# Six VectorE operations of a Mamba token in another order: three separate steps over two halves instead of one chain per half

## The chip, the core and the metric

The kernel runs on one core of a Trainium2 chip. The core has five engines, each with an in-order queue of its own: TensorE (matmuls into PSUM, called PE in the profile), VectorE (DVE), ScalarE (ACT), GpSimd (POOL) and SyncE (SP), which here only issues DMA transfers. Engines wait for each other by semaphores: an instruction at the head of a queue that must wait holds everything behind it on that engine. The time is the device time of one launch in microseconds. Before the change the median of three runs is 7580.34 us (7578.54 to 7589.2).

## The reference, cut to what matters

The input is an image batch of 2 x 128 channels x 128 x 128. Four layers follow each other: a Mamba layer (a 3x3 convolution, then a Mamba scan, group norm, SiLU, residual), a density gate, a second Mamba layer of the same kind, and a residual block of two 3x3 convolutions. The change is in the scan of the two Mamba layers. Each pixel has its 128 channels cut into 8 tokens of 16, and the scan runs over these 8 tokens for 32 inner channels with 16 states each:

```python
dt = jax.nn.softplus(jnp.einsum('nlr,dr->nld', dt, dt_proj_w) + dt_proj_b)
A = -jnp.exp(A_log)
dA = jnp.exp(dt[..., None] * A)
dBx = dt[..., None] * Bm[:, :, None, :] * xc[..., None]
def step(h, inp):
    a, b, c = inp
    h = a * h + b
    return (h, jnp.sum(h * c[:, None, :], axis=-1))
```

## The kernel before

`_program` (L1028) runs `_mamba`, `_gates`, `_mamba` and `_basic_block`. `_mamba` (L289) works through 64 tiles of 512 pixels (four image rows) for each layer, 128 in all. In a tile the 32 x 16 states of a pixel lie on 128 partitions in four blocks (NJ = 4), so a state tensor of one token is 128 x 4 x 512; it is handled in two halves (`jp` = 0 and 1) of 128 x 2 x 512.

For each token t of 1 to 7 four engines work together:

- `load` (L429, SP's queue) brings `ur` and `bcr` of the token from DRAM, replicated over partitions. `ur` has 3 buffers, `bcr` 5.
- `inject` (L442, GpSimd, L445) multiplies them into `h[t]`, what is added to the state. `h` has 4 buffers.
- `decay` (L447) forms the factor a: eight TensorE matmul instructions (L454) write the exponent of the two halves into two PSUM tiles called `set`, four into each, and ScalarE takes the exponential in place (L463), one instruction for each half. The pool `ps_set` (L298) has three such tiles, used in turn.
- `token` (L465, VectorE) does three operations for each half: L472 multiplies a by h[t-1], in place in the `set` tile; L473 multiplies that by the C part of `bcr` into `r`, which has two buffers; L477, left out for the last token, adds it to h[t]. All three read or write the `set` tile, and the last of them lets it go.
- `gather` (L485, TensorE, L492) sums `r` over the states into the PSUM tile `ys`; after four tokens `gate` (L501, VectorE, L505) takes it over, and `out` projects the result (L512). `spread` (L523, VectorE) takes the statistics of a finished tile.

In between run the first steps for tiles further ahead: convolution taps (L323), transposes (L339), projections (L350, L364, L400), the token's own part (L420), and on ScalarE their copies, the SiLU (L357) and the softplus (L368) with table loads.

The order in each queue is written out by hand: every step of tile k gets a position, k * 7 plus a constant of the list at L268 to L286 (one unit is a token), all steps are sorted by it, ties by the order in which they were put, and emitted (`put`, L554, to L597). `decay` of token t stands at t - 1.2, `token` at t - 1 for half 0 and t - 0.5 for half 1, `gather` at t + 0.35; the two gates at 3.79 and 7.39, the statistics at 12.5. Nothing else is changed about who waits for whom: the semaphores follow from which instruction reads and writes which buffer.

Of the kernel before, what the change touches and what calls it, by code (L numbers as in the profile page):

```python
# [27 lines left out]
ALU = mybir.AluOpType  # L28
# [3 lines left out]
P = 128  # L32
NT, FT = 8, 16
# [8 lines left out]
NS = ROWS * P  # L42
# [237 lines left out]
STORE_AT = -4.15  # L280
LOAD_AT, INJECT_AT = -3.7, -1.8
REP_AT = -1.2
SUM_AT = 0.35
D_AT = (1.25, 4.2)
V_AT = (3.79, 7.39)
# [3 lines left out]
def _mamba(tc, src, w, con, dst, scratch, stats, H):  # L289


    nc = tc.nc
# [11 lines left out]
    live = {}  # L304
# [157 lines left out]
        for x in a:  # L462
            nc.scalar.activation(x, x, AF.Exp)  # L463

    def token(k, t, jp):  # L465

        s = live[k]
        if jp == 0:
            s["r", t] = st.tile([P, NJ, NS], F32, tag="r", name="r", bufs=2)
        pt = s["a", t][jp]  # L470
        js = slice(2 * jp, 2 * jp + 2)
        nc.vector.tensor_tensor(pt, pt, s["h", t - 1][:, js, :], ALU.mult)  # L472
        nc.vector.tensor_tensor(  # L473
            s["r", t][:, js, :], pt, s["bc", t - 1][:, 1].unsqueeze(1).to_broadcast([P, 2, NS]), ALU.mult
        )
        if t < NT - 1:
            nc.vector.tensor_tensor(s["h", t][:, js, :], pt, s["h", t][:, js, :], ALU.add)  # L477

    def through(k, g):

# [73 lines left out]
    def put(k, at, f, *args):  # L554
        at = early.get((k, f, *args), k * SPAN + at)
        todo.append((at, len(todo), f, (k, *args)))


    for k in range(len(src) * ntile):
        if k * ROWS % BAND == 0:  # L560
            put(k, BAND_AT, band)
        for tap in range(9):
            put(k, CONV_AT[tap], conv, tap)
        put(k, TURN_AT, turn)
        for n in range(4):
            put(k, IN_AT[n], project, *divmod(n, 2))
        for name in ("xc", "zs"):
            put(k, SILU_AT, silu, name)
        for i in range(2):
            put(k, BC_AT[i], inout, i)  # L570
        for g in range(2):
            put(k, DT_AT[g], step, g)
        put(k, SOFTPLUS_AT, softplus)
        put(k, PROD_AT, product)
        put(k, U_AT, scaled)
        for g in range(2):
            put(k, OWN_AT[g], own, g)
        put(k, OWN_U_AT, own_u)
        put(k, STORE_AT, store)
        for t in range(NT - 1):  # L580
            put(k, LOAD_AT + t, load, t)
            put(k, INJECT_AT + t, inject, t)
        for t in range(1, NT):
            put(k, REP_AT + t, decay, t)
            for jp in range(2):
                put(k, t - 1 + jp / 2, token, t, jp)
            put(k, SUM_AT + t, gather, t)
        for g in range(2):
            put(k, D_AT[g], through, g)
            put(k, V_AT[g], gate, g)  # L590
        put(k, OUT_AT, out)
        put(k, STATS_AT, spread)
        put(k, KEEP_AT, keep)
# [434 lines left out]
def _program(ctx, tc, d, cols, out):  # L1028
# [7 lines left out]
    with tc.tile_pool(name="const", bufs=1) as cp, tc.tile_pool(name="wts", bufs=1) as wp:  # L1036
        cc = cols["const"]
        ct = cp.tile([P, cc["neghalf"][1]], F32, tag="ct", name="ct")
        nc.sync.dma_start(out=ct, in_=d["const"])
        con = {k: ct[:, a:b] for k, (a, b) in cc.items()}  # L1040
        w1 = cp.tile([P, CG], F32, tag="w1", name="w1")
        nc.sync.dma_start(out=w1, in_=d["w1t"])
        w2 = cp.tile([CG, 2 * P + P // 2], F32, tag="w2", name="w2")
        nc.sync.dma_start(out=w2, in_=d["w2b"])
        b1 = cp.tile([CG, 1], F32, tag="b1", name="b1")
        nc.sync.dma_start(out=b1, in_=d["b1"])
        wm = {"w1": w1, "w2": w2[:, :P], "b2": w2[:, P : 2 * P], "one": w2[:, 2 * P :]}

        y = [dram.tile([P, H, P], F32, tag=f"y_{b}", name=f"y_{b}") for b in range(B)]

        def layer(src, n):
            w = _layer_weights(nc, wp, {k: d[f"L{n}_{k}"] for k in ("conv", "fold", "alog", "keep")}, cols[n], con)
            stats = wp.tile([P, B, H // ROWS, 6], F32, tag="stats", name="stats")
            _mamba(tc, src, w, con, y, scratch, stats, H)
            return w, stats

        x = [d["x"][b] for b in range(B)]
        w, stats = layer(x, 0)
        _gates(tc, x, w, con, y, stats, wm, b1, d["up"], x2, H)
        w, stats = layer(x2, 2)  # L1060
        with tc.tile_pool(name="ps_n", bufs=1, space=PSUM) as pp:
            norm = [_norm(nc, npool, pp, w, con, stats, b) for b in range(B)]
# [44 lines left out]
```

## Time and profile before

| | us |
|---|---|
| median of three runs | 7580.34 |
| the profiled execution, its span from first to last instruction | 7571.5 |
| VectorE busy | 7011.8 (93%) |
| TensorE busy (matmuls) | 6319.0 (83%) |
| GpSimd busy | 5499.8 (73%) |
| ScalarE busy | 4282.3 (57%) |
| L472, L473, L477 on VectorE together | 6254.0 |

In the profile a group is one line of the kernel on one engine: output and inputs by tile name, shape, count, then the busy time in us and the mean of one in ns, then the time that the engine was idle just before such an instruction, and what ended most of it. A line of the order of time gives the start in us from the beginning of the span, the duration, engine, line and operation; a bracket behind it is the idle time ahead of it and what ended it. Durations on VectorE overlap a little at their ends, so starts are compared with starts. In a line of stretches each engine has its busy time in the order PE, PEld, VectorE, ScalarE, GpSimd; then come the granted TensorE clock as a share of full speed, the mean busy share of the 16 DMA engines and GB/s.

The first Mamba layer runs up to about 3300 us, the second from about 3600 to 6900 us.

### The profile page before, as it was taken

How to read it: one execution, taken by the hardware profiler on the slowest of the kernel's cores; microseconds unless marked ns; L12 is line 12 of the kernel's file. 1: busy time of each engine (PE TensorE's matmuls, PEld its weight loads, DVE VectorE, ACT ScalarE, POOL GpSimd, SP SyncE). 2: the span in 40 equal slices, each digit the busy share in tenths (PEclk: the TensorE clock that was granted, in tenths of full speed). 3: DMA queues.
4: the chain of work that ended last, by engine and by line, in shares of the span. 5: the costliest groups of instructions: out<-in, count | busy, mean ns of one | idle time of the engine just before them, and what ended most of it. 6: DMA issues, size and time to landing. Idle time of an engine off the chain costs nothing.

```text
span 7571.5 us, 89536 instructions
## 1 busy us (share of the span) xinstructions
PE 6319.0 (83%) x30416; PEld 2335.1 (31%) x30416; DVE 7011.8 (93%) x7114; ACT 4282.3 (57%) x4877; POOL 5499.8 (73%) x1783
## 2 busy tenths in 40 slices
PE   7888888888888888867788888888888888887994
PEld 2222222222222222224222222222222222223873
DVE  5999999999999999978699999999999999999986
ACT  5666666666656656545556666666656655662222
POOL 5878777877787778754578777877787778775541
PEclk8999999999999999978899999999999999997997
DMA  8999999999999999954799999999999999996604
GB/s 204 252 251 252 251 250 246 256 251 253 246 248 254 250 243 249 245 194 173 193 249 247 250 250 249 250 256 246 249 252 252 251 245 253 249 253 199 207 7 172
DMA packets 573738, 1769.80 MB, mean 234 GB/s; under 512 B 85568, under 2 KB 239712, under 8 KB 458208
## 3 DMA queue, kind: packets, MB, share of 16 engines
q1 hardware_dynamic: 568672, 1747.28, 88.1%
q10 hardware_dynamic: 4608, 16.78, 0.6%
q8 instruction: 242, 3.96, 0.2%
q14 instruction: 216, 1.77, 0.1%
HBM read 1552.83 MB, written 210.89 MB: 233 GB/s over the span
## 4 chain that ended last, share of the span: by engine, by line
DVE 41%; DMA 25%; PE 19%; issue 7%; ACT 5%; POOL 2%; SPq 1%; POOLq 0%; DVEq 0%; ACTq 0%
DMA bcr<-sb 19%; DVE set L472 14%; DVE h L477 12%; DVE r L473 12%; PE m L911 6%; DMA ur<-su 3%; PE one L350 2%; PE set L454 2%; ACT set L463 2%; PE ys L492 2%; PE one L400 2%; POOL h L445 2%; DVE v L505 1%; PE ys L483 1%; ACT xc L357 1%
## 5 line engine op out<-in xcount | busy, mean ns | idle before, releaser
L445 POOL TENSOR_TENSOR h<-ur,bcr 128x2048 f32<-128x2048 f32 x896 | 4060.7, 4539 | 1257.0 <-DMA bcr<-sb 1096.1
L472 DVE TENSOR_TENSOR set<-set,h 128x1024 f32<-128x1024 f32 x1792 | 2193.5, 1224 | 267.6 <-ACT set L463 165.4
L473 DVE TENSOR_TENSOR r<-set,bcr 128x1024 f32<-128x1024 f32 x1792 | 2194.5, 1225 | 61.5
L463 ACT ACTIVATE set<-set 128x1024 f32<-128x1024 f32 x1792 | 1745.9, 1006 | 870.0 <-PE set L454 856.6
L477 DVE TENSOR_TENSOR h<-set,h 128x1024 f32<-128x1024 f32 x1536 | 1866.0, 1215 | 28.1 <-POOL h L445 27.8
L454 PE MATMUL set<-dt,rep 32*128 32x512 f32 x7168 | 1402.9, 675 | 104.9 <-DVE h L477 98.1
L492 PE MATMUL ys<-r,ct 128*32 128x512 f32 x7168 | 1172.5, 635 | 36.4 <-DVE r L473 36.1
L323 PE MATMUL one<-band,conv 128*128 128x512 f32 x2304 | 1081.3, 605 | 21.9 <-DMA band<-in_x_dram 12.6
L454 PEld LDWEIGHTS set<-dt,rep 32*128 32x128 f32 x7168 | 405.1, 193 | 1002.3 <-issue 468.1
L400 PE MATMUL one<-xc,keep 128*64 128x512 f32 x1008 | 322.4, 723 | 462.1 <-ACT xc L357 355.5
L323 PEld LDWEIGHTS one<-band,conv 128*128 128x128 f32 x2304 | 406.6, 189 | 668.0 <-issue 596.8
L911 PE MATMUL m<-comb,u 128*128 128x256 f32 x2304 | 507.8, 381 | 46.0 <-DVE comb L904 44.8
L483 PE MATMUL ys<-t,ct 128*128 128x512 f32 x512 | 322.6, 716 | 252.3 <-DVE v L505 250.7
L911 PEld LDWEIGHTS m<-comb,u 128*128 128x128 f32 x2304 | 436.2, 190 | 117.3 <-issue 54.5
L492 PEld LDWEIGHTS ys<-r,ct 128*32 128x32 f32 x7168 | 181.2, 112 | 929.2 <-issue 759.6
L352 ACT ACTIVATE xc<-one,keep 128x512 f32<-128x512 f32 x252 | 173.4, 688 | 509.2 <-PE one L350 504.2
L374 POOL TENSOR_TENSOR u<-dt,xc 128x1024 f32<-128x1024 f32 x128 | 302.8, 2365 | 98.0 <-ACT dt L368 98.0
L420 PE MATMUL one<-prod,ct 128*128 128x512 f32 x504 | 280.8, 640 | 109.1 <-POOL prod L412 78.8
L350 PE MATMUL one<-y,w_in 128*128 128x512 f32 x504 | 341.1, 765 | 1.6 <-ACT xc L352 1.6
L463 ACT ACT_TABLE_LOAD x254 | 325.9, 1283 | 4.5
L427 POOL TENSOR_TENSOR t<-t,xc 128x1024 f32<-128x1024 f32 x128 | 302.4, 2363 | 10.0
L364 PE MATMUL one<-xc,w_dt 128*128 128x512 f32 x504 | 306.4, 692 | 2.7 <-ACT bc L407 2.7
(167 smaller groups left out, 5901.7 us busy)
## 6 DMA issues: line engine op xcount, KB each, us to landing
ur<-su SPq DMA_DIRECT2D x896, 896.0 KB, 11.5
bcr<-sb SPq DMA_DIRECT2D x896, 448.0 KB, 11.7
ur<-su SPq DMA_DIRECT2D x896, 128.0 KB, 11.1
su<-u SPq DMA_DIRECT2D x1024, 64.0 KB, 3.4
sb<-bc SPq DMA_DIRECT2D x256, 224.0 KB, 2.7
bcr<-sb SPq DMA_DIRECT2D x896, 64.0 KB, 11.0
y<-o SPq DMA_DIRECT2D x128, 256.0 KB, 9.3
band<-in_x_dram SPq DMA_DIRECT2D x28, 640.0 KB, 10.9
```

The source lines that it names most:

```text
L323: nc.tensor.matmul(py.rearrange("p (r w) -> p r w", r=ROWS), lhsT=w["conv"][:, tap, :], rhs=xb[:, r + kh : r + kh + ROWS, kw : kw + P], st ...
L350: nc.tensor.matmul(p, lhsT=w[("in", "z")[i]][:, g, :], rhs=s["y"], start=True, stop=True)
L400: nc.tensor.matmul(p[g * NQ * DS : (g + 1) * NQ * DS, :], lhsT=w[("xb", "xcm")[i]], rhs=s["xc"][:, g, :], start=True, stop=True,)
L445: nc.gpsimd.tensor_tensor(b, s["ur", t], s["bc", t][:, 0].unsqueeze(1).to_broadcast([P, NJ, NS]), ALU.mult)
L454: nc.tensor.matmul(a[j // 2][:, j % 2, :], lhsT=w["rep"][r, q, :], rhs=s["dt"][r, g, :], start=True, stop=True, tile_position=(r.start, 0),)
L463: nc.scalar.activation(x, x, AF.Exp)
L472: nc.vector.tensor_tensor(pt, pt, s["h", t - 1][:, js, :], ALU.mult)
L473: nc.vector.tensor_tensor(s["r", t][:, js, :], pt, s["bc", t - 1][:, 1].unsqueeze(1).to_broadcast([P, 2, NS]), ALU.mult)
L477: nc.vector.tensor_tensor(s["h", t][:, js, :], pt, s["h", t][:, js, :], ALU.add)
L483: nc.tensor.matmul(s["ys", g], lhsT=con["ident"], rhs=s["t1"][:, g, :], start=True, stop=False)
L492: nc.tensor.matmul(s["ys", g][a : a + NQ * DJ, :], lhsT=red[:, q, :], rhs=r[:, j, :], start=False, stop=(q == NQ - 1), tile_position=(0, a),)
L911: nc.tensor.matmul(m[:, n // 2, n % 2], lhsT=u[:, i, kw, :], rhs=v[:, i, :, kw : kw + P], start=(kw == 0), stop=(kw == 2),)
```

## The change

`token` is taken apart into three functions, `decayed` (the line of L472), `weighted` (L473) and `update` (L477). Each has its own positions for the two halves, so that the six operations of a token are spread over one token's time, and the `update` of half 1 falls behind the first operation of the next token. The operands, shapes and the number of operations stay. The `r` buffer of a token is now taken in `weighted`.

```diff
+TOKEN_AT = (("decayed", (0.0, 0.5)), ("weighted", (0.34, 0.84)), ("update", (0.67, 1.17)))
...
-    def token(k, t, jp):
+    def decayed(k, t, jp):
+
+        s = live[k]
+        pt = s["a", t][jp]
+        nc.vector.tensor_tensor(pt, pt, s["h", t - 1][:, 2 * jp : 2 * jp + 2, :], ALU.mult)
+
+    def weighted(k, t, jp):
 
         s = live[k]
         if jp == 0:
             s["r", t] = st.tile([P, NJ, NS], F32, tag="r", name="r", bufs=2)
-        pt = s["a", t][jp]
-        js = slice(2 * jp, 2 * jp + 2)
-        nc.vector.tensor_tensor(pt, pt, s["h", t - 1][:, js, :], ALU.mult)
         nc.vector.tensor_tensor(
-            s["r", t][:, js, :], pt, s["bc", t - 1][:, 1].unsqueeze(1).to_broadcast([P, 2, NS]), ALU.mult
+            s["r", t][:, 2 * jp : 2 * jp + 2, :],
+            s["a", t][jp],
+            s["bc", t - 1][:, 1].unsqueeze(1).to_broadcast([P, 2, NS]),
+            ALU.mult,
         )
-        if t < NT - 1:
-            nc.vector.tensor_tensor(s["h", t][:, js, :], pt, s["h", t][:, js, :], ALU.add)
+
+    def update(k, t, jp):
+
+        s = live[k]
+        h = s["h", t][:, 2 * jp : 2 * jp + 2, :]
+        nc.vector.tensor_tensor(h, s["a", t][jp], h, ALU.add)
...
             put(k, REP_AT + t, decay, t)
-            for jp in range(2):
-                put(k, t - 1 + jp / 2, token, t, jp)
+            for f, at in TOKEN_AT:
+                for jp in range(2):
+                    if f != "update" or t < NT - 1:
+                        put(k, t - 1 + at[jp], {"decayed": decayed, "weighted": weighted, "update": update}[f], t, jp)
             put(k, SUM_AT + t, gather, t)
```

## The prediction

> **What bounds the kernel now.** I read the page's engine rows and costliest groups first, then the waits, then the order of time on single engines in one Mamba tile. I write D, W and U for the three VectorE operations of a token half (L472, L473, L477), with the half (0 or 1) and the token: D0(3).
>
> ```profile
> PE 6319.0 (83%) x30416; PEld 2335.1 (31%) x30416; DVE 7011.8 (93%) x7114; ACT 4282.3 (57%) x4877; POOL 5499.8 (73%) x1783
> ...
> L472 DVE TENSOR_TENSOR set<-set,h 128x1024 f32<-128x1024 f32 x1792 | 2193.5, 1224 | 267.6 <-ACT set L463 165.4
> L473 DVE TENSOR_TENSOR r<-set,bcr 128x1024 f32<-128x1024 f32 x1792 | 2194.5, 1225 | 61.5
> ...
> L477 DVE TENSOR_TENSOR h<-set,h 128x1024 f32<-128x1024 f32 x1536 | 1866.0, 1215 | 28.1 <-POOL h L445 27.8
> ```
>
> VectorE is the busiest engine; 1792 / 14 = 128 tiles carry the three groups. It waits little. In all waits:
>
> ```profile
> PEld set L454 <- DVE h L477: 335.7, 346, 1.4
> ...
> DVE set L472 <- ACT set L463: 165.4, 185, 9.3
> ...
> PE set L454 <- DVE h L477: 98.1, 166, 4.0
> ```
>
> The columns are the total, the times and the longest. Two rows say that TensorE already waits 434 us in front of L454 for a U. Those matmuls write into the `set` ring of three PSUM tiles; U is the last reader of the tile that they want. This is the second loop of the stage: U ends, L454 fills the tile, ScalarE takes the exponential (L463), D reads it.
>
> Five consecutive tiles, by stretches, from D0(1) to D0(1), last 48.95, 51.42, 50.10, 50.89, 48.95; four make the repeating 201.37 us, 50.34 a tile. VectorE rows of the first (start, duration):
>
> ```profile
> 1029.64 1.23 DVE L472 TENSOR_TENSOR set<-set,h 128x1024 f32<-128x1024 f32 x1
> 1030.91 1.22 DVE L473 TENSOR_TENSOR r<-set,bcr 128x1024 f32<-128x1024 f32 x1
> 1032.05 1.21 DVE L477 TENSOR_TENSOR h<-set,h 128x1024 f32<-128x1024 f32 x1
> 1033.18 0.68 DVE L505 TENSOR_TENSOR v<-ys,zs 128x512 f32<-128x512 f32 x1
> ```
>
> W starts 1.26 after the D whose result it reads; the next operation starts 1.14 after W, 1.13 after U, 0.60 after a gate or a statistic. D leads by 0.13 too much. In this tile VectorE never waits: it is the bound. In the others the granted TensorE clock is lower and D0(6), D0(7) wait 0.8 to 1.1 for the exponential:
>
> ```profile
> 1029.64:1078.59 48.95, 42.06 (x181) 13.53 (x182) 48.47 (x45) 31.26 (x36) 39.62 (x11) 1.00 0.98 256
> 1078.59:1130.01 51.42, 45.48 (x183) 13.99 (x186) 48.72 (x44) 30.46 (x36) 40.20 (x13) 0.90 0.97 245
> ```
>
> (the last three columns are clock, DMA share and GB/s).
>
> **What is gained.** By the listed positions the new order on VectorE is D0(t) U1(t-1) W0(t) D1(t) U0(t) W1(t). Two pairs per tile stay dependent: in token 1 there is no U1 of a token before, in token 7 no U0, so W follows its D there. That is 12 shortened D per tile. What an operation behind a D that it doesn't depend on costs, this stage doesn't show. The nearest rows are in the last block, where 256-element operations on PSUM stand 0.33 apart:
>
> ```profile
> 7105.61 0.42 DVE L926 TENSOR_TENSOR sd<-m,c 128x256 f32<-128x256 f32 x1
> 7106.07 0.43 DVE L927 TENSOR_TENSOR sd<-m,c 128x256 f32<-128x256 f32 x1
> 7106.41 0.68 DVE L931 TENSOR_TENSOR Y<-m,sd 128x512 f32<-128x512 f32 x1
> ```
>
> Here L926 and L927 write the PSUM one of the two `sd` tiles. L927, into the same tile, starts 0.46 later; L931, which reads the other `sd` and writes Y, 0.34. So the extra 0.13 belongs to the same tile, not to writing PSUM, and the interleaved neighbour is of another tile: I take 1.13 (bounds 1.13 and 1.26). The Trainium skill speaks against it: VectorE: DVE Perf Modes, "The DRAIN you can't avoid" and "Rules for kernel authors", say that the flush comes after each operation whatever the chaining, so only the number of operations counts. By it the gain is 0; by the rows 12 x 0.13 = 1.56 a tile, 200 us in 128 tiles. The 1.26 against 1.14 in this trace decides for the rows.
>
> **What is lost: the ring.** No engine's operations change in number, no DMA is added. But U moves back. U0 ended 1.26 + 1.14 + 1.22 = 3.62 after its D0 began. Now it is the fifth of six: for tokens 2 to 7 1.13 + 1.13 + 1.14 + 1.13 + 1.22 = 5.75, for token 1 (with the gate between) 1.26 + 1.14 + 0.60 + 1.13 + 1.22 = 5.35. U1 likewise ends two operations later. Tile 2t+1 of the ring takes over tile 2t-2, so the second half of L454 for token t waits for U0(t-1), and everything queued behind it on TensorE waits too: output, convolution taps, projections, the gathers, the next L454.
>
> VectorE alone, token by token with these spacings: 6.40, 6.80, 6.80, 7.40 (gate), 6.80, 7.40 (statistic), 5.80 = 47.40, against 48.95. Now the loop, with TensorE's rows:
>
> ```profile
> 1032.22 2.32 PE L454 MATMUL set<-dt,rep 32*128 32x512 f32 x8
> 1034.47 2.05 PE L512 MATMUL po<-keep,v 128*128 128x128 f32 x16
> ...
> 1040.97 1.14 PE L454 MATMUL set<-dt,rep 32*128 32x512 f32 x8
> ...
> 1064.26 1.12 PE L350 MATMUL one<-y,keep 128*128 128x512 f32 x2
> ```
>
> *Place A, D0(3).* U0(1) ended at 1033.26 and L512 started 1.21 later; from there to the next L454 TensorE had 6.50 of work without a free stretch worth naming (L512, L420, L483, L323, L492). L463 starts 1.17 after L454, D 1.04 after L463: 2.21. From D0(1) the new D0(3) is therefore not before 5.35 + 1.21 + 6.50 + 2.21 = 15.27. VectorE alone would be there at 13.20: a new wait of 2.07. Before, the same chain gave 3.62 + 1.21 + 6.50 + 2.21 = 13.54, under VectorE's 14.73, so it cost nothing.
>
> *D0(4) to D0(6)* are VectorE's: 22.07, 29.47, 36.27. The same sum for them (U0(3) to D0(5): 5.75 + 1.1 + 4.4 + 2.2 = 13.4 against 14.2) leaves under 1 us free.
>
> *Place B, D0(7).* U0(5) ends at 29.47 + 5.75 = 35.22, TensorE goes on at 36.33 (1.11, as behind another blocked L454). Before, it went on at 1064.26; the rows on ScalarE after that:
>
> ```profile
> 1066.18 0.60 ACT L354 COPY zs<-one 128x512 f32<-128x512 f32 x1
> 1066.81 1.28 ACT L357 ACT_TABLE_LOAD   x1
> ...
> 1072.23 1.93 ACT L463 ACTIVATE set<-set 128x1024 f32<-128x1024 f32 x2
> ```
>
> The chain L350, copy, table load, silu, L400, copy, table load, exponential made D0(7) possible at 1072.23 + 1.04, 9.01 after L350. The copy stood behind two exponentials; now the first is long done, and it can start 1.15 after L350 instead of 1.92: 8.24 remain. D0(7) is at 44.57, VectorE alone 43.67: a wait of 0.90. Then 5.80 to the next D0(1): 50.37, which is 47.40 + 2.97, and 1.42 longer than the 48.95.
>
> In a tile of lower clock TensorE is at L454 for token 6 some 35.5 after the start (5.6 behind the gate's L483, as now), so D0(6) is 37.7 and not 36.3; L454 to L454 takes 7.9 as now, D0(7) 46.6, the next tile 52.4, against 51.42: +1.0. For the two others the same way gives +1.1 to +1.2. The mean over four is (1.42 + 1.0 + 1.1 + 1.2) / 4 = 1.18.
>
> **The sum.** 128 x 1.18 = 151 us. The profiled execution's span is 7571.5, and 8.8 lie between it and the median shown, 7580.34; so 7571.5 + 151 + 8.8 = **7731 us**.
>
> **What stays covered.** W1 is the last reader of `bcr` and moves one operation back, 1.1 us. The loads at L439 already wait for L473 (222.9 us, 201 times, on SP's queue); behind them queue all other transfers, and GpSimd's L445 waits for those. VectorE waits for L445 only 27.8 us at U, and U now comes two operations later in the token, which covers it. Uncovered it would be 201 x 1.1 = 221 us. The gate before token 1's D1 needs the gather of token 7, which ends about 0.8 before it; with a halved matmul speed it would be level.
>
> **Rivals.** *The saving without the loss (faster).* TensorE would have to reach D0(3)'s tile 2.07 sooner and D0(7)'s 0.90 sooner than I sum, by work that now only looks contiguous. Then the tile is 50.34 - 1.56 = 48.78, and the time 7580 - 200 = **7380**. For it: VectorE's 93% and L472's only 165 us behind L463. Against: the 434 us of waiting in front of L454, which show a ring without room. It decides from the point where the two new waits together fall under 1.56. A DMA floor wouldn't stop it: the share is 0.97 to 0.98 in these stretches and 1.03 when full, 50.34 x 0.975 / 1.03 = 47.7.
>
> *No shorter D (the change doesn't do what it says).* With 1.26 kept, the same working gives 15.40 for D0(3), 45.48 for D0(7) and 51.41 for the tile, +2.46; at lower clock about +2. 128 x 2.1 = 270: **7850**.
>
> *Even.* The saving and the waits cancel, because a TensorE that idles longer is granted more clock and the tiles of 51 us lose their own waits: about **7580**.
>
> **How the numbers follow.** My forecast has 0.68, with its own range of 7650 to 7820; no shorter D 0.12; even 0.07, of which 0.05 within 0.2% (15 us, about what this kernel's measurement can tell from no change) and the rest split; the faster rival 0.13. The range leaves out the faster rival and little at the top: 7570 to 7870. Faster 0.14, same 0.05, slower 0.81.
>
> **What would show it.** Right: W no longer 1.26 behind D and spacings of 1.13 to 1.14; L472's idle time behind L463 up from 165 to some 400 us, 2 us at the third token and 1 at the seventh; TensorE's waits before L454 for L477 about doubled; VectorE's share down to about 88% ((7011.8 - 200) / 7722). Wrong: D still followed at 1.26 (the row of the last block misled me), or no new wait at token 3 (TensorE had hidden room), or a wait for L445 (the `bcr` buffers weren't covered).

## The result, and the profile after

The changed kernel takes 8079.57 us (median of four runs, 8075.57 to 8082.96) against 7584.77 for the kernel before on the same chip: a ratio of 1.0644, 95% interval 1.0626 to 1.0662. The profiled execution has a span of 8081.2 us, 509.7 more than before. The forecast had the direction (slower, 0.81) and the hold that causes the loss, but only 151 us of it, without the slower clock behind the hold; 7731 us and even the end of the range, 7870, are far below.

The page of the changed kernel, engine rows and groups (D is L470 here, W L477, U L488, the exponent matmuls L455, their exponential L464):

```profile
PE 6909.9 (86%) x30416; PEld 2647.5 (33%) x30416; DVE 6895.7 (85%) x7114; ACT 4310.1 (53%) x4877; POOL 5484.3 (68%) x1783
...
L470 DVE TENSOR_TENSOR set<-set,h 128x1024 f32<-128x1024 f32 x1792 | 2196.7, 1226 | 966.0 <-ACT set L464 867.0
...
L477 DVE TENSOR_TENSOR r<-set,bcr 128x1024 f32<-128x1024 f32 x1792 | 2178.1, 1215 | 8.8
L455 PE MATMUL set<-dt,rep 32*128 32x512 f32 x7168 | 1755.6, 711 | 447.1 <-DVE h L488 431.3
L488 DVE TENSOR_TENSOR h<-set,h 128x1024 f32<-128x1024 f32 x1536 | 1864.5, 1214 | 5.0 <-POOL h L446 5.0
```

VectorE works less (6895.7 against 7011.8) and waits more: D stood 267.6 us idle before, 966.0 now, 867.0 of it for the exponential. The second thing is on TensorE's row: the same 30416 matmuls are busy 6909.9 us instead of 6319.0. They have become slower; the mean granted TensorE clock of the run is 0.864 of full speed, before 0.929.

The order of time on VectorE in one tile (start, duration; idle time ahead in the bracket). The tile begins at 1157.11 with D0(1):

```profile
1160.12 1.22 DVE L470 TENSOR_TENSOR set<-set,h 128x1024 f32<-128x1024 f32 x1
1161.25 1.22 DVE L488 TENSOR_TENSOR h<-set,h 128x1024 f32<-128x1024 f32 x1
...
1169.17 1.21 DVE L477 TENSOR_TENSOR r<-set,bcr 128x1024 f32<-128x1024 f32 x1
1174.02 1.23 DVE L470 TENSOR_TENSOR set<-set,h 128x1024 f32<-128x1024 f32 x1 [3.63 <-ACT set L464]
```

D is now followed 1.13 later (1160.12 to 1161.25), as taken from the `sd` rows. D0(3) waits 3.63, and this is the picture of every one of the ten tiles between 1047.89 and 1594.02: they all last 54.61 or 54.62, with D waiting 3.63 at token 3, 0.84 at token 5, 0.86 or 0.87 at token 7 and 1.41 or 1.42 at the next tile's token 1. The reason stands on TensorE, in the same tile:

```profile
1159.69 1.13 PE L455 MATMUL set<-dt,rep 32*128 32x512 f32 x4
1162.61 1.13 PE L455 MATMUL set<-dt,rep 32*128 32x512 f32 x4 [1.79 <-DVE h L488]
1163.67 3.52 PE L523 MATMUL po<-keep,v 128*128 128x128 f32 x16
1166.98 1.23 PE L421 MATMUL one<-prod,ct 128*128 128x512 f32 x2
...
1171.80 1.14 PE L455 MATMUL set<-dt,rep 32*128 32x512 f32 x8
```

and in the kernel before:

```profile
1034.47 2.05 PE L512 MATMUL po<-keep,v 128*128 128x128 f32 x16
1036.36 1.02 PE L420 MATMUL one<-prod,ct 128*128 128x512 f32 x2
```

The second half of L455 for token 2 waits 1.79 us for U0(1), the hold of the forecast. But what comes behind it, L523 (the output projection, L512 before), needs 3.31 us to the next start where before it was 1.89. In stretches:

```profile
1160.20:1163.60 3.40, 1.61 (x8) 0.33 (x4) 3.40 (x5) 1.19 (x2) 3.40 (x2) 1.00 0.29 64
1163.60:1167.00 3.40, 3.40 (x19) 3.33 (x18) 3.40 (x4) 1.01 (x1) 2.26 (x1) 0.56 1.03 275
...
1177.30:1180.70 3.40, 2.12 (x9) 0.63 (x8) 3.40 (x4) 1.01 (x1) 3.32 (x3) 1.00 0.85 244
1180.70:1184.10 3.40, 3.40 (x6) 1.45 (x5) 3.40 (x4) 1.01 (x1) 3.40 (x2) 0.55 0.93 239
```

A stretch of 3.4 us in which TensorE was busy 1.61 or 2.12 is followed by one with the clock at about a half. The hold itself is short; much of the price is paid behind it, when the matmuls that it delayed run at half speed. The second pair is the hold at token 4 (1.28 us on TensorE), in front of convolution taps.

### The profile page after: what moved, and what is told of

Same layout as the page of the kernel before. It is cut to its first block, busy times and chain, and to the rows that moved or that the text cites. A ratio compares the mean times of both kernels' runs of the same rounds, so it can differ in the third digit from the quotient of the medians.

```text
span 8081.2 us, 91072 instructions
## 1 busy us (share of the span) xinstructions
PE 6909.9 (86%) x30416; PEld 2647.5 (33%) x30416; DVE 6895.7 (85%) x7114; ACT 4310.1 (53%) x4877; POOL 5484.3 (68%) x1783
## 4 chain that ended last, share of the span: by engine, by line
PE 40%; DVE 18%; DMA 14%; issue 11%; POOL 9%; ACT 7%; SPq 2%; POOLq 0%; DVEq 0%; ACTq 0%
PE set L455 10%; DMA ur<-su 9%; POOL h L446 8%; PE one L324 7%; DVE h L488 7%; DVE set L470 6%; PE m L924 6%; PE ys L503 4%; ACT set L464 3%; PE one L351 3%; DVE r L477 3%; DMA bcr<-sb 3%; PE po L523 3%; PE one L401 2%; PE one L365 2%
## 5 line engine op out<-in xcount | busy, mean ns | idle before, releaser
L446 POOL TENSOR_TENSOR h<-ur,bcr 128x2048 f32<-128x2048 f32 x896 | 4049.5, 4541 | 140.3 <-DMA bcr<-sb 109.9
L470 DVE TENSOR_TENSOR set<-set,h 128x1024 f32<-128x1024 f32 x1792 | 2196.7, 1226 | 966.0 <-ACT set L464 867.0
L464 ACT ACTIVATE set<-set 128x1024 f32<-128x1024 f32 x1792 | 1771.5, 1007 | 1219.4 <-PE set L455 886.2
L477 DVE TENSOR_TENSOR r<-set,bcr 128x1024 f32<-128x1024 f32 x1792 | 2178.1, 1215 | 8.8
L455 PE MATMUL set<-dt,rep 32*128 32x512 f32 x7168 | 1755.6, 711 | 447.1 <-DVE h L488 431.3
L488 DVE TENSOR_TENSOR h<-set,h 128x1024 f32<-128x1024 f32 x1536 | 1864.5, 1214 | 5.0 <-POOL h L446 5.0
L324 PE MATMUL one<-band,conv 128*128 128x512 f32 x2304 | 1294.3, 705 | 22.6 <-DMA band<-in_x_dram 13.0
L503 PE MATMUL ys<-r,ct 128*32 128x512 f32 x7168 | 1077.4, 674 | 1.9 <-DVE r L477 1.9
L455 PEld LDWEIGHTS set<-dt,rep 32*128 32x128 f32 x7168 | 487.7, 197 | 1510.0 <-issue 1054.3
L413 POOL TENSOR_TENSOR prod<-bc 128x512 f32<-128x512 f32 x128 | 162.2, 1268 | 1091.4 <-ACT bc L408 943.8
L324 PEld LDWEIGHTS one<-band,conv 128*128 128x128 f32 x2304 | 479.8, 223 | 808.4 <-issue 728.0
L401 PE MATMUL one<-xc,keep 128*64 128x512 f32 x1008 | 276.8, 628 | 264.2 <-ACT xc L358 261.1
L523 PE MATMUL po<-keep,v 128*128 128x128 f32 x2048 | 446.3, 408 | 1.3 <-DVE v L516 1.3
L523 PEld LDWEIGHTS po<-keep,v 128*128 128x128 f32 x2048 | 409.5, 306 | 100.9 <-issue 98.2
L503 PEld LDWEIGHTS ys<-r,ct 128*32 128x32 f32 x7168 | 148.3, 113 | 791.0 <-issue 781.4
L365 PE MATMUL one<-xc,w_dt 128*128 128x512 f32 x504 | 403.3, 893 | 2.7 <-ACT bc L408 2.7
L333 ACT ACTIVATE yc<-one,keep 128x512 f32<-128x512 f32 x128 | 88.2, 689 | 456.1 <-PE one L324 456.1
```

The costliest lines, as they stand in the source:

```text
L324: nc.tensor.matmul(py.rearrange("p (r w) -> p r w", r=ROWS), lhsT=w["conv"][:, tap, :], rhs=xb[:, r + kh : r + kh + ROWS, kw : kw + P], st ...
L365: nc.tensor.matmul(p, lhsT=w["dt"], rhs=s["xc"][:, g, :], start=True, stop=True)
L446: nc.gpsimd.tensor_tensor(b, s["ur", t], s["bc", t][:, 0].unsqueeze(1).to_broadcast([P, NJ, NS]), ALU.mult)
L455: nc.tensor.matmul(a[j // 2][:, j % 2, :], lhsT=w["rep"][r, q, :], rhs=s["dt"][r, g, :], start=True, stop=True, tile_position=(r.start, 0),)
L470: nc.vector.tensor_tensor(pt, pt, s["h", t - 1][:, 2 * jp : 2 * jp + 2, :], ALU.mult)
L477: nc.vector.tensor_tensor(s["r", t][:, 2 * jp : 2 * jp + 2, :], s["a", t][jp], s["bc", t - 1][:, 1].unsqueeze(1).to_broadcast([P, 2, NS]), ...
```

## The experiments

Each is a change to the kernel after the change, unless it says before. Four chips were used, and each ratio is against the kernel before on the same chip: 7565.65 us for e1 to e4, 7578.86 for e5 to e8, 7573.93 for e9 to e12 and 7578.65 for e13.

### Is it the late U, and does TensorE's queue make it dear?

**The exponent matmuls of the two halves apart (e1_split).** In the emitted order of TensorE and ScalarE half 1 moves 0.3 of a token back, so that L523 and others no longer stand behind it.

```diff
-REP_AT = -1.2
+REP_AT = (-1.2, -0.9)
...
-    def decay(k, t):
+    def decay(k, t, jp):    # one set tile, its two blocks, one exponential
...
-            put(k, REP_AT + t, decay, t)
+            for jp in range(2):
+                put(k, REP_AT[jp] + t, decay, t, jp)
```

> The changed kernel with the exponent matmuls of a token (decay) cut into two steps: half 0 stays at t - 1.2, half 1 goes to t - 0.9 in TensorE's and ScalarE's order, so that other matmuls stand between them and no longer behind a half that waits for a late U. Theory (the wait for U0 in the ring holds TensorE's whole queue, and its clock drops after each hold): VectorE's shortened operations then count, no wait at the third token, a tile of 47.5 to 49.5 us instead of 54.6, granted clock back above 0.92, 7220 to 7450 us. Rival 1 (the later release of bcr starves the loads): the tile stays at 54 us or so, 7950 to 8080. Rival 2 (the ring itself is too small, wherever the matmuls stand): little comes back, 7800 to 8000.

Measured: 7556.95 us, ratio 0.9991 (0.9975 to 1.0006), clock 0.912. The whole loss is gone, with VectorE's order as in the change. D0(3) waits 0.7 or less in most tiles instead of 3.63. So the hold in TensorE's queue costs the 500 us, and both rivals (starved loads, a ring too small wherever the matmuls stand) fall. But it isn't faster than before; the expected 7220 to 7450 was missed, and so was a clock above 0.92. The mean clock alone doesn't give the time: 0.912 here and 0.929 before take equally long. The missing gain is taken up below.

**The late U alone (e2_late_u).** VectorE's order D0 W0 D1 W1 U0 U1: nothing of a neighbouring token, both W directly behind their D, U0 as late as in the change.

```diff
-TOKEN_AT = (("decayed", (0.0, 0.5)), ("weighted", (0.34, 0.84)), ("update", (0.67, 1.17)))
+TOKEN_AT = (("decayed", (0.0, 0.4)), ("weighted", (0.1, 0.5)), ("update", (0.7, 0.8)))
```

> The changed kernel with VectorE in the order D0 W0 D1 W1 U0 U1 within a token: nothing of the neighbouring token between, both W directly behind their D (no shortening), but U0 as late as in the change. Theory (the late U is the cause): as slow as the change or slower, 8050 to 8300 us, TensorE blocked in front of the second half, the clock at 0.83 to 0.88. Rival (the mixing with the neighbouring token is the cause, not the late U): near the kernel before, 7560 to 7650.

Measured: 8504.1 us, ratio 1.124 (1.1195 to 1.1286), clock 0.847; D0(3) waits 4.99, the tile is 58.03. More than expected, on the theory's side: without any of the gain and with U0(1) later still, the loss is larger. The mixing with the neighbouring token is not what costs. (D1 is also one operation earlier in this order, so not all of the surplus is U's.)

**U less late (e7_ddwuwu).** The order D0 D1 W0 U0 W1 U1 has no operation directly behind one whose result it reads, and U0 is fourth and U1 sixth, where the change has fifth and eighth (counted from D0 of their token).

```diff
+TOKEN_AT = (("decayed", (0.0, 0.17)), ("weighted", (0.34, 0.67)), ("update", (0.5, 0.84)))
```

> The changed kernel (exponent matmuls unsplit) with the order D0 D1 W0 U0 W1 U1 within a token: no operation directly behind one whose result it reads, but U0 fourth and U1 sixth, 0.1 to 1.1 us earlier than in the change. Theory (the time follows the hold): chain U0(1) to D0(3) 5.22 + 1.21 + 6.5 + 2.21 = 15.1 at full clock against VectorE's 14.2, place B no longer late; shorter holds, fewer half-clock windows: 7400 to 7800. Rival (any order that isn't the old chain costs the same): 8000 to 8100.

Measured: 7573.4 us, ratio 0.9997 (0.9987 to 1.0007), clock 0.925. With U0 one place earlier and U1 two, the 500 us are gone; D0(3) waits 0.87 or less in about half of the tiles and 1 to 2.9 in the others, so the hold is shorter here, not gone.

**More bcr buffers (e4_bcr6).** SP's wait in front of the bcr load (L440) for W had risen from 222.9 to 1842.9 us, which looks like a cause.

```diff
-        m = s["bc", t] = st.tile([P, 2, NS], F32, tag="bcr", name="bcr", bufs=5)
+        m = s["bc", t] = st.tile([P, 2, NS], F32, tag="bcr", name="bcr", bufs=6)
```

> The changed kernel with six bcr buffers instead of five. Theory (the waits of SP for L477 are a consequence, not the cause): 8060 to 8090 us. Rival (bcr, released one operation later by W1, holds up the loads): 7600 to 7950, and SP's waits for L477 gone.

Measured: 8073.65 us, ratio 1.0671 (1.0626 to 1.0716), clock 0.866. SP's wait for W falls to 73.3 us and the time stays, within the theory's 8060 to 8090: the wait for a bcr buffer is a consequence of the late VectorE, not the cause.

### Is it the clock, and does it fall because of the hold?

**Filling the hold (e3_fill).** TensorE writes half 0 of tokens 2 and 4 three times, the same values, ahead of the half that must wait: 2048 more matmul instructions.

```diff
-        for j in range(NJ):
+        for j in ([0, 1] * 2 if t in (2, 4) else []) + list(range(NJ)):
```

> The changed kernel; for tokens 2 and 4 TensorE writes half 0 of the exponent three times instead of once (same result), so that part of the hold in front of half 1 is filled with matmuls. Theory (the granted clock drops because TensorE stands idle there): although there are more matmuls, the half-clock windows behind these two holds go, L523 takes 2 us instead of 3.5, the tile loses 1.5 to 3.4 us, 7650 to 7890. Rival (the clock follows the load or the program as a whole): the clock stays at 0.86 or falls and the time is 8080 to 8200.

Measured: 7773.5 us, ratio 1.0275 (1.0233 to 1.0316), clock 0.94. More work on TensorE, and 300 us less time than the 8073.65 of e4_bcr6, which stands for the change on the same chip. The order of time on TensorE behind the filled hold:

```profile
1063.76 2.84 PE L455 MATMUL set<-dt,rep 32*128 32x512 f32 x12
1067.08 1.13 PE L455 MATMUL set<-dt,rep 32*128 32x512 f32 x4 [0.47 <-DVE h L488]
1068.13 2.05 PE L523 MATMUL po<-keep,v 128*128 128x128 f32 x16
1070.02 1.02 PE L421 MATMUL one<-prod,ct 128*128 128x512 f32 x2
```

The second half still starts only when U0(1) is done (0.47 of the hold is left), and L523 is back at 1.89 to the next start. This tile began at 1061.59, and the stretch of all of it reads:

```profile
1061.59:1112.63 51.04, 47.18 (x197) 15.64 (x198) 47.51 (x44) 31.10 (x36) 39.78 (x12) 1.00 0.92 253
```

At full clock its D0(3) is 15.26 after D0(1), waiting 2.00. The forecast's chain had 15.27 and 2.07.

**The same number of matmuls behind the hold (e13_fill_behind).** For the same tokens half 1 is written three times instead of half 0.

```diff
-        for j in range(NJ):
+        for j in list(range(NJ)) + ([2, 3] * 2 if t in (2, 4) else []):
```

> The changed kernel with as many extra matmuls as e3_fill and for the same tokens 2 and 4, but repeating half 1, behind the hold instead of in it (same result). Theory (the clock falls because TensorE stands idle in the hold; what fills the hold keeps it up): the hold stays empty, clock 0.85 to 0.90, no gain, 8060 to 8350 us. Rival (more matmuls anywhere keep the clock up): clock above 0.92 and 7700 to 7900, as e3_fill.

Measured: 8934.34 us, ratio 1.1797 (1.1749 to 1.1845), clock 0.83. As many matmuls as in the run before, and 1161 us between them. The hold stays empty (1.80 us), the half-clock stretch behind it now lasts twice as long (1048.6 to 1055.4), part of the repeated matmuls and L523 run in it, and they lengthen the chain to D0(3), whose wait is 6.22. The theory's ceiling of 8350 was too low; that more matmuls anywhere keep the clock up is refuted. (The repeats would lengthen this chain at full clock too, so not all of the loss over the change is the clock's.)

### Where did the gain of VectorE go?

With the hold gone or shortened, three forms end at 7557 to 7573, none below the kernel before, although their VectorE has less to do. Two attempts to get more out of the split:

**Half 0 earlier (e5_split13)**, `REP_AT = (-1.3, -0.9)`, so that token 7's stands ahead of a projection that waits for the SiLU.

> The split of e1_split with half 0 a little earlier, at t - 1.3 instead of t - 1.2 (half 1 stays at t - 0.9): for token 7 half 0 then stands ahead of the projection that waits for the SiLU. Theory (what is left in e1_split, waits of 0.5 to 1.5 us at the seventh token and at the next tile's first, comes from TensorE standing idle behind that projection and its half clock afterwards): those waits shrink, tile 48 to 49 us, 7300 to 7480. Rival (the loads are the limit by now, DMA share 0.97): no gain over e1_split, 7530 to 7590.

Measured: 7569.57 us, ratio 0.9992 (0.9976 to 1.0007). The wait at token 7 is gone as meant; in its place D0(1) of the next tile waits 1.9 to 2.8 for its exponential. The time is the rival's; that the loads are what limits this form was not tested on it.

**The split in the kernel before (e6_before_split13)**, with VectorE's old order, and **the split with D0 D1 W0 U0 W1 U1 (e8_ddwuwu_split13)**, both at (-1.3, -0.9).

> The kernel before, with the same split of the exponent matmuls (t - 1.3, t - 0.9) and VectorE's old order. Theory (the old order has 48.95 us of VectorE's work in a tile, and only its 1.4 us of waits can go): 7390 to 7560, and e5_split13 faster than this one by up to 200 us, the worth of the shortened operations. Rival (the split is what helps, the new order is worth nothing even without the hold): this one as fast as e5_split13 or faster.

> e7_ddwuwu with the split of the exponent matmuls (t - 1.3, t - 0.9). Theory: hold gone, but D1 now needs its exponential two operations earlier, so the late half 1 is what it waits for: 7400 to 7700. Rival (the split costs nothing in this order): 7250 to 7400.

Measured: 7660.96 (1.0119, 1.0097 to 1.0141) and 7605.73 (1.0044, 1.0028 to 1.0059). For the old order the split is a loss, which wasn't expected; e5_split13 is 1.2% faster than it, so the new order is worth something in this frame, though some of the 1.2% may be the fixed tile of 51.20 us that this run alone of the two falls into (last section). For D0 D1 the split is a small loss too, within the expected 7400 to 7700.

**Fewer loads.** The `ur` loads of tokens 2 and 5 are left out in three kernels: the order D0 D1 W0 U0 W1 U1 (e9_ddwuwu_less), the kernel before (e10_before_less), and the change (e12_after_less). Every engine does the same operations, on other data.

```diff
+        if t in (2, 5):
+            s["ur", t] = s["ur", t - 1]
+        else:
...              # the two ur loads as before
```

> e7_ddwuwu without the ur loads of tokens 2 and 5 (their inject takes the ur of the token before, so the output is another; every engine does the same operations), about 2 of 13 MB a tile less. Theory (e1_split, e5_split13 and e7_ddwuwu all end at 7557 to 7574 us because the replicated loads, 250 GB/s at a share of 0.97, are the next limit): the saving of VectorE shows, 7200 to 7430 us. Rival (the loop through TensorE and ScalarE is what limits them): 7530 to 7580.

> The kernel before without the same ur loads. Theory (VectorE with its 48.95 us a tile and the half-clock windows bound it, the loads only little): 7450 to 7580, above e9_ddwuwu_less by 100 to 300 us. Rival (before is bound by the loads): as fast as e9_ddwuwu_less.

> The changed kernel without the ur loads of tokens 2 and 5. Theory (the hold of the ring and the clock set its time, not the loads): 8030 to 8090. Rival (the loads play a part in the 500 us): 7600 to 7950.

Measured: 7430.42 (0.9816, 0.9798 to 0.9835), 7530.61 (0.9947, 0.993 to 0.9963) and 8074.16 (1.0666, 1.0641 to 1.069). The first is at the very edge of what was expected. Each against its full form: the order D0 D1 W0 U0 W1 U1 gains some 140 us, the kernel before 43 (against its 7573.93), the change nothing clear of noise. The stretch from 600 to 3200 us, in the order D0 D1 W0 U0 W1 U1 with all loads, then with fewer:

```profile
600.00:3200.00 2600.00, 2340.16 (x9182) 755.63 (x9177) 2443.43 (x2219) 1610.41 (x1809) 2060.55 (x596) 0.95 0.97 251
```

```profile
600.00:3200.00 2600.00, 2364.72 (x9340) 768.12 (x9338) 2497.86 (x2272) 1630.59 (x1827) 2100.67 (x607) 0.96 0.76 213
```

The last but one number is the DMA share, 0.97 against 0.76. So behind VectorE's bound lay the loads, a little below it: with all of them the shortened operations are worth nothing, with fewer they are worth 7530.61 - 7430.42 = 100 us, less than half of the 233 that all 14 D of a tile in 128 tiles come to at 0.13 us a piece. Where the rest goes is not shown: D's named wait stays the exponential (252.0 us, with all loads 387.7), so the loop through TensorE still takes a part, and by which wait the loads act was not followed. The hold, where it stands, hides even the 100 us: the change with fewer loads is where it was.

**The store earlier (e11_ddwuwu_store)**, to fill the dip of the DMA share once a tile: `STORE_AT` -4.8 instead of -4.15 in the order D0 D1 W0 U0 W1 U1.

> e7_ddwuwu with the store of u and B, C ahead of the last load of the tile before instead of behind it (STORE_AT -4.8 instead of -4.15; all work is done). Theory (part of the floor is the dip in the DMA share once a tile, when the next loads wait for the store to land): the last load fills the dip, 7350 to 7530. Rival (the queue waits longer for GpSimd's u in front of the store): 7560 to 7700.

Measured: 7610.8 (1.005, 1.0033 to 1.0066). It is the rival that came: it costs half a per cent, and the store's wait for GpSimd's u has grown from 66.0 to 467.2 us.

No form that does all the work beats the kernel before; three equal it.

## Why the prediction was right or wrong

**The gain: right.** The next operation starts 1.13 behind a D that it doesn't depend on, at the two dependent pairs of a tile still 1.26 or so (1207.83 to 1209.08, 1157.11 to 1158.38). The waits of a tile sum to 3.63 + 0.84 + 0.86 + 1.42 = 6.75, which leaves 54.61 - 6.75 = 47.86 for VectorE's 47.40. The rule of the Trainium skill that was set against the rows (VectorE: DVE Perf Modes, "The DRAIN you can't avoid"), taken alone, would have left the 1.26. The same section also says that a next operation that is not held starts earlier, which the forecast passed over; it gives no time for that, and the 1.13 is this trace's.

**The hold: right as a mechanism, exact at full clock.** D0(2) came at 6.40 as summed. In the tile of e3_fill in which the clock stayed up, D0(3) came at 15.26.

**The step that failed** is the term of work inside the chains: "from there to the next L454 TensorE had 6.50 of work". It was taken at the full-clock durations of the trace before, and kept for a kernel that holds TensorE in front of it. With the change, from L523 to the next L455 it is 8.13 (1163.67 to 1171.80). Token by token, in the tile that begins at 1157.11:

| | forecast | after | what lies in it |
|---|---|---|---|
| D0(1) to D0(3) | 15.27 | 16.91 | L523 3.31 instead of 1.89 |
| D0(3) to D0(5) | 14.20 | 15.21 | six tap matmuls 4.46 to the next start |
| D0(5) to D0(7) | 15.10 | 15.19 | |
| D0(7) to D0(1) | 5.80 | 7.30 | L455 3.28, L365 2.08, L503 1.92 |
| tile | 50.37 | 54.61 | |

For the last row the full-clock durations of the same eight, two and eight matmuls before were 1.14, 1.12 and 1.50 (1070.22, 1071.29, 1072.35). Nearly all of the missing 4.24 us lies where the clock is near a half. Of it 2.65 is behind the two holds. The 1.50 of the last row is behind another pause, that of L401 for the SiLU, which the forecast's place B had in its chain but followed by full clock:

```profile
1200.36 1.08 PE L401 MATMUL one<-xc,keep 128*64 128x512 f32 x4 [2.05 <-ACT xc L358]
1201.37 3.28 PE L455 MATMUL set<-dt,rep 32*128 32x512 f32 x8
```

The mean of 1.18 a tile should have been 54.61 - 50.34 = 4.27; times 128 that is 547 us, somewhat more than the measured 509.7; the tiles at the ends of the layers, which are not of these kinds, were not followed.

**The case called even had the sign wrong.** It supposed "a TensorE that idles longer is granted more clock". The page TensorE: Matmul & The Clock Gate of the Trainium skill, "Why this matters for your kernels", says that a pause of more than about 3 us between bursts brings the clock down; in this trace 1.79 and 1.28 us of hold were enough, in stretches of 3.4 us with TensorE 1.61 and 2.12 busy. But the length of the pause does not decide alone. In the kernel before the same pause of 2.83 us for the SiLU stands in two tiles that follow each other, and the matmuls behind it run at full clock in one and at half in the other:

```profile
1069.21 1.08 PE L400 MATMUL one<-xc,keep 128*64 128x512 f32 x4 [2.83 <-ACT xc L357]
1070.22 1.14 PE L454 MATMUL set<-dt,rep 32*128 32x512 f32 x8
...
1119.78 1.98 PE L400 MATMUL one<-xc,keep 128*64 128x512 f32 x4 [2.83 <-ACT xc L357]
1121.69 2.09 PE L454 MATMUL set<-dt,rep 32*128 32x512 f32 x8
```

Nor does TensorE's busy time in the stretch ahead: 1.96 us from 1067.76 to 1071.17 brought no drop there, 2.12 did in the change. What decides stays open: the forecast could have named the half clock as a risk of its holds, but these traces give no rule to sum it by.

**Covered work: right in effect.** VectorE waits for L446 at U only 5.0 us; the bcr buffers cost nothing (e4_bcr6). **The faster rival's floor was too low:** 47.7 us a tile for the loads, from a share of 1.03 when full, counted the dip of every tile as room, and the one attempt to use it (e11_ddwuwu_store) failed. The runs without this hold and with all loads stay at 50 to 51 us. No form with all loads came near 7380.

**What was to show it:** D's wait behind the exponential rose not to 400 but to 867. TensorE's named wait for U didn't double (458.3 us over its two rows, before 433.8); the hold shows in single tiles by its bracket, and in the weight loads' idle time without a named releaser, 468.1 before and 1054.3 now.

## What to carry to other kernels

When operations on one engine are reordered, price the release of each buffer as well as the spacing: an operation that is the last reader of a ring's tile holds the queue of the engine that refills it, with everything behind. Where the held engine is TensorE, add its clock: matmuls timed in a trace without a hold are not the price of the same matmuls behind one. And before a gain on the busiest engine is counted, look for what stands just below it; here a saving of 233 us on VectorE came to nothing with all loads (7573.4 us against 7578.86 in e7_ddwuwu) and to 100 us with fewer.

## What the runs showed of the hardware that was not expected

- Two short holds in a tile, 1.79 and 1.28 us, are followed by half-clock stretches; 2048 extra matmuls inside the holds raised the mean clock from 0.864 to 0.94 and saved some 300 us, the same number behind them lowered it to 0.83 and cost 855 (8934.34 - 8079.57).
- The tile fell into step with the clock. The half-clock stretches of the change are 3.4 us long or twice that (1164.0 to 1167.4, 1201.6 to 1208.4), at the same places in each tile, and all 37 tiles from 900 to 3000 us last 54.60 to 54.62 us, which is 16 x 3.413. With six bcr buffers or fewer loads the length is the same. The late U has 58.03 (17 x 3.413), the matmuls behind the hold 61.44 (18 x 3.413), and the split in the kernel before, which runs at nearly its old time, 51.20 (15 x 3.413). The kernel before and the three forms that equal it have no such length; most of their tiles lie between 48 and 54. So in four different kernels the tile settled at a whole number of these stretches. The step up to the next whole number may then be part of a loss; no run separates it from the hold.
